# Entry of the first batch, order of the last batch and PReLU on Pool in a four-layer fused kernel

## The chip, the cores and the metric

One core of a Trainium2 chip runs the whole program. Its engines are PE (TensorE, matmuls), DVE (VectorE), ACT (ScalarE), POOL (GpSimd) and SP (SyncE, which here issues DMAs). The metric is the time of the device for one execution in microseconds, from the first to the last instruction on that core. Three runs are given for the kernel before, and one more execution was profiled.

## The reference

The input is 8 images of 512 channels and 32 x 32 = 1024 pixels, in fp32. Four layers follow each other, all of 1x1 convolutions:

```python
# layer 0: attention normalised by the largest singular value
f_x = relu(batchnorm(conv1x1(x, Wf, bf))); g_x = relu(batchnorm(conv1x1(x, Wg, bg)))
h_x = conv1x1(x, Wh, bh)                          # 64 channels each; batch statistics
attn = einsum('bcn,bcm->bnm', f_x, g_x) / sigma   # sigma: largest singular value
x = conv1x1(einsum('bnm,bcm->bcn', attn, h_x), Wv, bv) + x
# layer 1: group norm, softmax attention over 1024 pixels, 512 channels, residual
# layer 2: softmax attention with 128 channels, a batch norm, residual
# layer 3: signs of x times signs of W
y = einsum('bchw,oc->bohw', sign(x + rsign_bias), sign(W) * mean(abs(W)))
s = batchnorm(y) + x
t = s - pr_shift
out = where(t > 0, t, pr_slope * t) + pr_bias     # PReLU
```

## The kernel before

A tile of x is 128 partitions x 4 channel blocks (`cc`) x 1024 pixels; a "half" is 512 pixels. One fp32 matmul of the program shows as two instructions in the trace.

**Start (lines 1128 to 1187).** For each image the loop loads x in four blocks, and PE multiplies it by the weights of f, g and h (`products(i, cc)`, with i = 0, 1, 2; line 1157). For the first image the loop goes over the blocks and, in each, over f, g and h; for the others over f, g, h and then the blocks. x has two buffers, so the load of image b+2 waits for PE's work on image b. The small row tensors (`bg_row`, `bvc`, `bhc`, `wv2`, lines 194 to 204) are loaded by POOL's queue at the very beginning. The weights are loaded by SP's queue between the images.

**Middle (about 97 to 201 us).** The singular values come from a chain of small products (`chain`), and `filler()` yields other PE work in small items (weight products, transposes, Gram matrices) that are put between its steps. PE's order here is written out by hand (`manual_schedule`). At its end `entering(0)` brings in the first batch of the second part: `enter` yields after each of four channel blocks (matmul L396, then on DVE L405 and the statistics L408, L409), then after the two products of the group norm (L416, L423). Two filler items are put after each of the four blocks, and six after each of the other two steps. The last filler item is the product L1197 that makes `wo`.

**Entry.** The pools of the first part are closed, the pool `late` is opened (its tile `ones2` is filled by a DVE memset, L1375), then `normal` (lines 435 to 447) normalises the first batch, by halves, on DVE and ACT in turn; `split_h` makes differences of it on DVE (L312 to L315), and `make_u` multiplies (L373). A big product is done in the seven-product form of Strassen and Winograd (`seven`): sums and differences of quarters, seven products and additions of results. In it the first product is copied out of its bank by ACT (L335) before the fifth may accumulate onto that bank. Then `sums_of` makes the sums of quarters of `wo` and of the layer-2 weights on DVE.

**Batches (`fast`, lines 826 to 927).** Eight times: layer-1 scores (`scores1`), values, layer 2 (`project2`, `scores2`, `values2`, `close2`), layer 3 (`leave`). Steps of the next batch fill the gaps. `inverse_sums` sums the exponentials by a matmul with `ones2` (L788), takes the reciprocal on DVE (L796) with one half on each side of 64 partitions, and spreads it by four DMAs (L800); two more bring a row of it into `guard`, whose values `count_bad` examines on DVE (L737 to L747) at the end; the verdict `bad` decides whether a general path is run. In `leave` each output block takes a PSUM eviction with the residual (L700, DVE), a Relu (L704, ACT), a scaling with a bias (L705, ACT), a sum (L712, DVE) and the DMA to the output (L715, SP). The last batch takes the two signs of the weights unpacked (`signs`), has no next batch to fill its gaps, and ends the program.

Order of the engines: apart from PE's hand-written stretch, a scheduler places the instructions of each engine in a queue, which then runs in that order.

Of the kernel before, what the change touches and what calls it, by code (L numbers as in the profile page):

```python
# [83 lines left out]
def kernel(  # L84
# [109 lines left out]
    bg_row = const.tile([P, P], F32, tag="bg_row", name="bg_row")  # L194
    nc.gpsimd.dma_start(out=bg_row, in_=rows[MID + C :].partition_broadcast(P))

    bvc = const.tile([P, CC], F32, tag="bvc", name="bvc")
    nc.gpsimd.dma_start(out=bvc, in_=rows[MID : MID + C].rearrange("(cc p) -> p cc", p=P))
    bhc = const.tile([P, 1], F32, tag="bhc", name="bhc")
    wv2 = const.tile([P, C], F32, tag="wv2", name="wv2")  # L200
    for i in range(2):
        both = side(i)
        nc.gpsimd.dma_start(out=bhc[both, :], in_=rows[0:MID].rearrange("(p o) -> p o", o=1))
        nc.gpsimd.dma_start(out=wv2[both, :], in_=w_v0)
    minus_half = const.tile([P, CC], F32, tag="minus_half", name="minus_half")
# [36 lines left out]
    sa3 = const.tile([P, CC], F32, tag="sa3", name="sa3")  # L242
    cb3 = const.tile([P, CC], F32, tag="cb3", name="cb3")
    inv2 = const.tile([P, CC], F32, tag="inv2", name="inv2")
    bb2 = const.tile([P, CC], F32, tag="bb2", name="bb2")
# [49 lines left out]

    def sums_of(a, more):

        a11, a12, a21, a22 = a
        s1, s2, s4 = more
        tt = nc.vector.tensor_tensor  # L300
        tt(s1, a21, a22, ALU.add)
        tt(s2, s1, a11, ALU.subtract)  # L302
        tt(a21, a11, a21, ALU.subtract)
        tt(s4, a12, s2, ALU.subtract)
        return {"A11": a11, "A12": a12, "A22": a22, "S1": s1, "S2": s2, "S3": a21, "S4": s4}
# [128 lines left out]

    def normal(env, xt, by_halves=False):

        sc, bi = norm
        ht = env["big"].tile([P, CC, N], F32, tag="h", name="h")
        for ns in [half(h) for h in range(NH)] if by_halves else [slice(0, N)]:
            for cc in range(CC):  # L440
                s1, b1 = sc[:, cc : cc + 1], bi[:, cc : cc + 1]
                hs, xs = ht[:, cc, ns], xt[:, cc, ns]
                if cc % 2:
                    nc.scalar.activation(hs, xs, AF.Identity, bias=b1, scale=s1)
                else:
                    nc.vector.tensor_scalar(hs, xs, s1, b1, ALU.mult, ALU.add)
        return ht
# [214 lines left out]
    def leave(env, xt, dst, halves=range(NH), signs=None, stop=False):  # L662
# [3 lines left out]
        for h in halves:  # L666
# [7 lines left out]
            for j in range(CC // 2):  # L674
# [15 lines left out]
                if signs is None:  # L690
                    ps = product(sw3)
                    nc.scalar.activation(y2, ps, AF.Identity, bias=round3, scale=1.0 / PACK)
                    nc.vector.tensor_scalar(y2, y2, ROUND, None, ALU.subtract)
                    nc.vector.scalar_tensor_tensor(y1, y2, -PACK, ps, ALU.mult, ALU.add)
                    sums = y1, y2
                else:
                    sums = [product(lt) for lt in signs]

                for y, ps, oc in ((y1, sums[0], j), (y2, sums[1], j + 2)):
# [3 lines left out]
                    up = small.tile([P, HF], F32, tag="half_a", name="up3")  # L703
                    nc.scalar.activation(up, y, AF.Relu, bias=cb3[:, oc : oc + 1])  # L704
                    nc.scalar.activation(  # L705
                        y,
                        y,
                        AF.Identity,
                        bias=pb3[:, oc : oc + 1],
                        scale=col("L3_conv_pr_slope", oc),  # L710
                    )
                    nc.vector.scalar_tensor_tensor(  # L712
                        y, up, ps3[:, oc : oc + 1], y, ALU.mult, ALU.add
                    )
                    nc.sync.dma_start(out=dst[:, oc, half(h)], in_=y)  # L715
                yield
# [12 lines left out]
    def count_bad(env):  # L729
# [6 lines left out]
        nbad = late.tile([g, 1], F32, tag="nbad", name="nbad")  # L736
        nc.vector.tensor_scalar(fine, guard, 1.0 / GUARD, None, ALU.is_gt)  # L737
        nc.vector.tensor_scalar(other, guard, GUARD, None, ALU.is_lt)
        nc.vector.tensor_tensor(fine, fine, other, ALU.mult)
# [44 lines left out]
    def inverse_sums(env, esum, row):  # L784
# [21 lines left out]
        return full  # L806

    def entering(n):

# [16 lines left out]
    def fast(env, n, hb, ua):  # L826
# [14 lines left out]
        for k, _ in enumerate(scores1(env, hb, ua, es)):  # L841
            if rest3 and k % 2 == 0:
                if next(rest3[0], "end") == "end":
                    rest3.pop()
                    if more and order[n + 1] not in resident:
                        resident[order[n + 1]] = load_x(order[n + 1])
            if k == 8 and more:
                ahead = entering(n + 1)
# [57 lines left out]
        values2(0, range(0, 2))  # L906
        r = inverse_sums(env, esum, B + n)
        values2(0, range(2, NTH))
        att = values2(0, range(NTH, NT))
        values2(1, range(0, NTH))  # L910
        close2(xt, att, 0)
        att = values2(1, range(NTH, NT))
        count = iter(()) if more else count_bad(env)
        next(count, None)
        fill()
        for _ in leave(env, xt, dst, [0], signs):
            fill()
        close2(xt, att, 1)
        rest3.append(leave(env, xt, dst, [1], signs, more))
        if more:  # L920
            next(rest3[0])
        fill(2)
        for _ in steps:
            pass
        if not more:
            for _ in rest3.pop():
                next(count, None)

# [146 lines left out]
    def scale_signs(total):  # L1075
# [28 lines left out]
        nc.vector.tensor_tensor(pb3, slope, cb3, ALU.mult)  # L1104
        nc.vector.tensor_tensor(pb3, pb3, vec("L3_conv_pr_bias"), ALU.add)

    def scale_z():
# [39 lines left out]
    for b in range(B):  # L1147
        xt = load_x(b) if b else first
        for name, src, pool in later.get(b, ()):
            load_w(name, src, shapes.get(name, [P, CC, C]), pool)  # L1150
        if b >= B - 2:
            resident[b] = xt
# [12 lines left out]
        if b == 0:  # L1165
            for cc in range(CC):
                for i in range(3):
                    products(i, cc)
        for i in range(3):
            if b == B - 1 and i == 2:  # L1170
                for _ in natural("q", "w3"):
                    pass
            if b:
                for cc in range(CC):
# [182 lines left out]
    with tc.manual_schedule(engines={mybir.EngineType.PE}):  # L1357
# [7 lines left out]
        for k in range(CC + 2):  # L1365
            next(steps)
            for _ in range(2 if k < CC else 6):
                next(todo, None)
# [3 lines left out]

    late = ctx.enter_context(tc.tile_pool(name="late", bufs=1))
    ones2 = late.tile([P, P], F32, tag="ones2", name="ones2")
    nc.vector.memset(ones2, 1.0)  # L1375
    guard = late.tile([2 * B * 4, NH, P], F32, tag="guard", name="guard")
    bad = late.tile([1, 1], I32, tag="bad", name="bad")

    with ExitStack() as main:
# [9 lines left out]
        ua = got[0]  # L1389
        weights["o"] = sums_of(quarters_of(wo, chunks, cols2), [so[:, i] for i in range(3)])  # L1390
        sp = late.tile([P, 3, 2, P], F32, tag="sp", name="sp")
        tp = quarters_of(sbw["tpg"], chunks, [slice(0, P), slice(P, 2 * P)])
        weights["tp"] = sums_of(tp, [sp[:, i] for i in range(3)])
        for n in range(B):
# [172 lines left out]
```

## Time and profile before

| | us |
|---|---|
| median of three runs | 1938.97 (1938.92 to 1940.28) |
| span of the profiled execution | 1940.4 |
| PE busy | 1909.5 |
| DVE busy | 1149.8 |
| ACT busy | 513.6 |
| POOL busy | 224.1 |
| first matmul starts | 4.35 |
| last sign product ends on PE | 1928.8 |
| last DVE instruction ends | 1935.2 |

A line of the timeline gives the start, the duration, the engine, the line, the operation, output<-input, shape and count; in brackets stands the idle time of the engine before it and what ended that. A line of the waits gives engine, own line, what it waited for, the total, the number of times and the longest. Busy PE includes matmuls at half rate, so it must also be asked how far apart matmuls start.

### The profile page before, as it was taken

What the parts mean: (1) busy time and instruction counts of PE and PEld (TensorE: products, weight loads), DVE (VectorE), ACT (ScalarE), POOL (GpSimd) and SP (SyncE); (2) the same over time, 40 slices, a digit from 0 to 9 for tenths busy, and PEclk for the clock granted to TensorE, in tenths of its full rate; (3) what the DMA queues carried; (4) which work ended last, traced back from release to release, by engine and by line L of the source; (5) the groups of instructions that cost most, each with busy time, mean ns of one, the idle gap of its engine ahead of it and who ended that gap; (6) DMA issues with size and microseconds to landing.
All of it is one profiled execution on the core that took longest, in us unless ns stands there. A gap on an engine that the chain in (4) does not pass through costs nothing.

```text
span 1940.4 us, 16698 instructions
## 1 busy us (share of the span) xinstructions
PE 1909.5 (98%) x6230; PEld 984.6 (51%) x6230; DVE 1149.8 (59%) x1867; ACT 513.6 (26%) x815; POOL 224.1 (12%) x176
## 2 busy tenths in 40 slices
PE   8999999999999999999999999999999999999997
PEld 2367447544655447454555446544645455544653
DVE  2255578448864587637754677348663775466545
ACT  2141222124221432025212331034202421133014
POOL 1000001200112001200111011201120011101120
PEclk9999999999999999999999999999999999999999
DMA  8420000002000110002000120002000200010001
GB/s 308 163 77 7 1 6 12 1 11 87 17 1 1 33 65 17 1 10 89 15 2 1 33 71 11 1 11 87 11 0 1 86 14 9 0 33 22 11 1 57
DMA packets 27289, 67.00 MB, mean 35 GB/s; under 512 B 3824, under 2 KB 4592, under 8 KB 26560
## 3 DMA queue, kind: packets, MB, share of 16 engines
q1 hardware_dynamic: 26112, 65.09, 9.9%
q8 instruction: 51, 0.84, 0.2%
q0 software_dynamic: 224, 0.33, 0.1%
q10 hardware_dynamic: 864, 0.43, 0.1%
q14 instruction: 38, 0.31, 0.1%
HBM read 38.51 MB, written 18.87 MB: 30 GB/s over the span
## 4 chain that ended last, share of the span: by engine, by line
PE 89%; DVE 8%; ACT 1%; issue 1%; DMA 0%; ACTq 0%; POOL 0%; DVEq 0%
PE bank L373 40%; PE bank L540 20%; PE bank L890 6%; PE bank L767 6%; PE bank L1157 4%; PE bank L641 3%; PE bank L396 2%; PE bank L658 1%; PE wide L1197 1%; PE bank L944 1%; DVE both L712 1%; DVE both L700 1%; PE bank L945 1%; PE bank L788 1%; PE wide L1244 1%
## 5 line engine op out<-in xcount | busy, mean ns | idle before, releaser
L540 PE MATMUL bank<-e,vt 128*128 128x512 f32 x768 | 334.0, 593 | 0.0
L540 PEld LDWEIGHTS bank<-e,vt 128*128 128x128 f32 x768 | 145.2, 190 | 175.2 <-issue 173.0
L373 PE MATMUL bank<-ut,h 128*128 128x512 f32 x384 | 181.3, 596 | 0.0
L330 DVE TENSOR_TENSOR e<-bank,e 128x512 f32<-128x512 f32 x128 | 87.7, 685 | 65.2 <-PE bank L373 64.5
L373 PE MATMUL bank<-us,hs 128*128 128x512 f32 x256 | 122.1, 599 | 1.3 <-DVE us L302 0.5
L373 PEld LDWEIGHTS bank<-ut,h 128*128 128x128 f32 x384 | 71.6, 190 | 85.7 <-issue 83.5
L890 PE MATMUL bank<-e,tpg 128*128 128x512 f32 x256 | 114.6, 596 | 0.0
L767 PE MATMUL bank<-tpg 128*128 128x512 f32 x256 | 114.6, 592 | 0.0
L774 ACT ACTIVATE e<-bank 128x512 f32<-128x512 f32 x128 | 76.4, 597 | 128.6 <-PE bank L767 128.6
L373 PE MATMUL bank<-h,wu 128*128 128x512 f32 x192 | 90.7, 594 | 2.2 <-ACT ut L335 1.5
L345 POOL TENSOR_TENSOR e<-e 128x512 f32<-128x512 f32 x32 | 44.0, 1375 | 419.6 <-ACT e L324 419.6
L373 PE MATMUL bank<-wo,h 128*128 128x256 f32 x384 | 91.8, 382 | 0.0
L779 DVE TENSOR_TENSOR esum<-esum,e 128x1024 f32<-128x1024 f32 x48 | 58.8, 1225 | 54.8 <-ACT e L774 54.8
L330 DVE TENSOR_TENSOR vt<-bank,vt 128x512 f32<-128x512 f32 x64 | 44.1, 689 | 70.5 <-PE bank L373 70.1
L890 PEld LDWEIGHTS bank<-e,tpg 128*128 128x128 f32 x256 | 48.0, 190 | 63.9 <-issue 63.9
L767 PEld LDWEIGHTS bank<-tpg 128*128 128x128 f32 x256 | 48.6, 190 | 60.7 <-issue 60.5
L373 PEld LDWEIGHTS bank<-wo,h 128*128 128x128 f32 x384 | 71.6, 190 | 13.4 <-ACT vt L324 4.1
L345 POOL TENSOR_TENSOR ut<-ut 128x512 f32<-128x512 f32 x16 | 21.8, 1360 | 483.0 <-ACT ut L326 483.0
L373 PEld LDWEIGHTS bank<-us,hs 128*128 128x128 f32 x256 | 46.8, 190 | 56.0 <-issue 46.3
L669 ACT ACTIVATE sg<-xt,rb 128x512 f16<-128x512 f32 x64 | 45.2, 718 | 104.4 <-DVE xt L660 100.9
L796 DVE RECIPROCAL rsum<-bank 128x512 f32<-128x512 f32 x16 | 53.7, 3358 | 30.3 <-PE bank L788 30.3
L1157 PE MATMUL bank<-xt,fg 128*64 128x512 f32 x256 | 60.3, 616 | 4.4 <-DMA fg<-in_w_fg 4.4
(320 smaller groups left out, 3080.4 us busy)
## 6 DMA issues: line engine op xcount, KB each, us to landing
xt<-in_x SPq DMA_DIRECT2D x55, 512.0 KB
out<-both SPq DMA_DIRECT2D x64, 256.0 KB
rfull<-rsum SPq DMA_DIRECT2D x64, 128.0 KB
f_dram<-f SPq DMA_DIRECT2D x8, 256.0 KB
fb<-f_dram SPq DMA_DIRECT2D x8, 256.0 KB
w<-in_w SPq DMA_DIRECT2D x1, 1024.0 KB
q<-in_w_q SPq DMA_DIRECT2D x1, 1024.0 KB
k<-in_w_k SPq DMA_DIRECT2D x1, 1024.0 KB
```

Source lines behind the costliest of these rows:

```text
L330: nc.vector.tensor_tensor(dst, ps, u, ALU.add)
L345: nc.gpsimd.tensor_tensor(c22, c22, c12, ALU.add)
L373: mm(out=ps[:, q * w : (q + 1) * w], lhsT=lt(ka, kb, q, k), rhs=rhs(ka, kb, q, k), start=first and q == 0 and k == 0, stop=last and k == 1 ...
L540: mm(out=ps, lhsT=a[:, t, bass.ts(r_, P)], rhs=e[t], start=first and t == 0, stop=last and t == NTH - 1, skip_group_check=True,)
L641: mm(out=ps[:, i, :], lhsT=xt[:, cc, bass.ts(4 * h + i, P)], rhs=sbw["tpg"][:, cc, 2 * P : 3 * P], start=cc == 0, stop=cc == CC - 1,)
L669: nc.scalar.activation(sg[:, cc, :], xt[:, cc, half(h)], AF.Sign, bias=rb3[:, cc : cc + 1])
L767: mm(out=ps, lhsT=pt[:, 0, bass.ts(t, P)], rhs=tt[:, 0, half(h)], start=True, stop=True,)
L774: nc.scalar.activation(e[:, half(h)], ps, AF.Exp, scale=float(P) ** -0.5)
L779: nc.vector.tensor_tensor(esum, esum, e, ALU.add)
L796: nc.vector.reciprocal(r, ps)
L890: mm(out=banks[h], lhsT=gt[:, t, :], rhs=es[t][:, half(h)], start=t == 0, stop=t == NT - 1,)
L1157: mm(out=banks[i][side(h), :], lhsT=w0[i][:, cc, :], rhs=xt[:, cc, half(h)], start=cc == 0, stop=cc == CC - 1,)
```

## The change

1. For the first image PE does all f and g products before the h products.
2. The row loads, except `bhc`, move from POOL's queue at the start to SP's queue at image 4.
3. At the entry, three filler items instead of two stand after each channel block, five instead of six after the other two steps; `normal` for the first batch runs on DVE alone; the `late` pool waits for single tiles of the memory it takes over and no longer for the whole; `sums_of` for `wo` and for the layer-2 weights moves into the first batch's `scores1`, after its steps 2 and 6.
4. The last batch: the reciprocals are taken for all 128 partitions in two instructions (`inverse_rows`), without the spreading DMAs; the second half's products, the closing of the halves, the guard count and the two halves of `leave` stand in another order.
5. Of the last batch's eight outputs, six take PReLU as a maximum with `nc3` = -`cb3` times `ps3` (one DVE instruction), a scaling with bias `qb3` on ACT, and a sum on POOL. The seventh stays; the eighth is done and stored in two quarters.

The core of the diff:

```diff
-    nc.gpsimd.dma_start(out=bg_row, in_=rows[MID + C :].partition_broadcast(P))
-    nc.gpsimd.dma_start(out=bvc, in_=rows[MID : MID + C].rearrange("(cc p) -> p cc", p=P))
-        nc.gpsimd.dma_start(out=wv2[both, :], in_=w_v0)
+    def load_rows():
+        nc.sync.dma_start(out=bg_row, in_=rows[MID + C :].partition_broadcast(P))
+        nc.sync.dma_start(out=bvc, in_=rows[MID : MID + C].rearrange("(cc p) -> p cc", p=P))
+        for i in range(2):
+            nc.sync.dma_start(out=wv2[side(i), :], in_=w_v0)
...
-                if cc % 2:
+                if cc % 2 and not alone:
                     nc.scalar.activation(hs, xs, AF.Identity, bias=b1, scale=s1)
                 else:
                     nc.vector.tensor_scalar(hs, xs, s1, b1, ALU.mult, ALU.add)
...
+                    if signs is not None and (h == 0 or j == 0):
+                        nc.vector.tensor_scalar(
+                            up, y, nc3[:, oc : oc + 1], ps3[:, oc : oc + 1], ALU.max, ALU.mult
+                        )
+                        nc.scalar.activation(
+                            y, y, AF.Identity, bias=qb3[:, oc : oc + 1],
+                            scale=col("L3_conv_pr_slope", oc),
+                        )
+                        nc.gpsimd.tensor_tensor(y, y, up, ALU.add)
+                        nc.sync.dma_start(out=dst[:, oc, half(h)], in_=y)
+                        continue
+                    final = signs is not None and y is y2
+                    for q in (slice(0, HF // 2), slice(HF // 2, HF)) if final else [slice(0, HF)]:
...
+    def inverse_rows(env, esum, row):
+        full = env["small"].tile([P, NH, HF], F32, tag="rfull", name="rfull", bufs=1)
+        for h in range(NH):
+            ps = bank()
+            mm(out=ps, lhsT=ones2, rhs=esum[:, half(h)], start=True, stop=True)
+            nc.vector.reciprocal(full[:, h, :], ps)
...
+            if n == 0 and k == 2:
+                weights["o"] = sums_of(quarters_of(wo, chunks, cols2), [so[:, i] for i in range(3)], True)
+            if n == 0 and k == 6:
+                tp = quarters_of(sbw["tpg"], chunks, [slice(0, P), slice(P, 2 * P)])
+                weights["tp"] = sums_of(tp, [sp[:, i] for i in range(3)], True)
...
+            r = inverse_rows(env, esum, B + n)
+            att = values2(0, range(2, NT))
+            values2(1, range(0, 2))
+            close2(xt, att, 0)
+            values2(1, range(2, 6))
+            before, after = leave(env, xt, dst, [0], signs), leave(env, xt, dst, [1], signs)
+            count = count_bad(env)
+            next(count)
+            next(before)
+            next(before)
+            att = values2(1, range(6, NT))
+            next(before)
+            close2(xt, att, 1)
+            for _ in before:
+                pass
+            next(after)
+            next(count)
+            for _ in after:
+                pass
...
+        nc.vector.tensor_scalar(nc3, cb3, -1.0, None, ALU.mult)
+        nc.vector.tensor_tensor(qb3, cb3, vec("L3_conv_pr_bias"), ALU.add)
...
+        if b == 4:
+            load_rows()
...
         if b == 0:
             for cc in range(CC):
-                for i in range(3):
+                for i in range(2):
                     products(i, cc)
...
-            if b:
+            if b or i == 2:
                 for cc in range(CC):
                     products(i, cc)
...
-            for _ in range(2 if k < CC else 6):
+            for _ in range(3 if k < CC else 5):
                 next(todo, None)
...
-    late = ctx.enter_context(tc.tile_pool(name="late", bufs=1))
+    late = ctx.enter_context(tc.tile_pool(name="late", bufs=1, reuse_waits="tile"))
```

## The prediction

> **What bounds the kernel.** I read the page's busy table and slices first, then the list of waits of PE, then the timeline at three places. PE is busy 98% of the span, so a change can gain only where PE stands still, where it runs slowly, or behind its last matmul.
>
> ```profile
> span 1940.4 us, 16698 instructions
> PE 1909.5 (98%) x6230; PEld 984.6 (51%) x6230; DVE 1149.8 (59%) x1867; ACT 513.6 (26%) x815; POOL 224.1 (12%) x176
> PE   8999999999999999999999999999999999999997
> ...
> PE bank L1157 <- DMA fg<-in_w_fg: 4.4, 1, 4.4
> PE bank L416 <- DVE mv L415: 3.5, 5, 1.8
> PE bank L396 <- ACT pv L282: 1.6, 4, 0.7
> PE bank L373 <- ACT ut L335: 1.5, 1, 1.5
> PE bank L1157 <- DMA h<-in_w_h: 1.4, 1, 1.4
> PE bank L681 <- ACT sg L669: 1.1, 1, 1.1
> ...
> PE bank L373 <- DVE h L446: 0.7, 1, 0.7
> ```
>
> PE's idle time is 1940.4 - 1909.5 = 30.9 us. The first slice (8) and the last (7) hold most of it; the named waits are each a microsecond or two. All lie at the start, at the entry of the first fast batch (180 to 206 us) or in the last batch: the three places which the diff edits.
>
> The start, PE and its weight loads:
>
> ```profile
> 4.35 4.30 PE L1157 MATMUL bank<-xt,fg 128*64 128x512 f32 x8 [4.35 <-DMA fg<-in_w_fg]
> 10.02 1.98 PE L1157 MATMUL bank<-xt,h 128*64 128x512 f32 x4 [1.37 <-DMA h<-in_w_h]
> ...
> 10.02 0.30 PEld L1157 LDWEIGHTS bank<-xt,h 128*64 128x64 f32 x4 [3.05 <-DMA h<-in_w_h]
> ```
>
> The page's 1.37 us understates this: the weight loads stop for 3.05 us, and matmul ends are modelled. Eight instructions follow each other every 0.43 us (4.35 to about 7.8), then PE waits for h until 10.02. From 10.02 the spacing is again 0.43 us, until about 14.0; then it is 0.215 us. So PE runs at half rate twice.
>
> The end:
>
> ```profile
> 1919.88 3.60 PE L658 MATMUL bank<-att,z 128*128 128x512 f32 x8
> 1926.10 0.67 DVE L660 TENSOR_TENSOR xt<-bank,xt 128x512 f32<-128x512 f32 x1
> 1927.99 2.73 DVE L700 SCALAR_TENSOR_TENSOR both<-bank,sa,xt 128x512 f32<-128x512 f32 x4 [1.16 <-PE bank L681]
> 1934.47 0.75 DVE L712 SCALAR_TENSOR_TENSOR both<-up,ps,both 128x512 f32<-128x512 f32 x1 [0.71 <-ACT both L705]
> ```
>
> PE finishes the second half's L658 products at 1923.5, but DVE adds the last of them only at 1926.1-1926.8, since it stands behind L700, L712 and the guard count. The last matmul ends at 1928.8, the last DVE instruction at 1935.2, and 5.2 us of output DMA and closing follow.
>
> [...]Here L345 takes 1.26 us on POOL and a comparable add on DVE (L330) 0.69. [...]the trace has 0.41 us (L446) against 0.69.[...]
>
> **Part by part.** The base is the profiled span of 1940.4; the three timed runs are 1938.92 to 1940.28, so I subtract the sum from the median 1938.97.
>
> *Start.* The f and g products of all four channel blocks come first, h last. PE has 16 f/g products (32 instructions) before it needs h, landed by 10.02. From 4.35 it goes on at 0.43 us;[...] First case: 9 slow instructions, 39 at 0.215 = 8.4, end 16.7. Second: 14 slow, 34 fast = 7.3, end 17.8. Before, batch 0 ended at 20.5. Gain 2.7 to 3.8; I take 3.2. It needs x on time: the windowed traffic sums to about 1.6 MB by 8 us and 2.3 MB by 11, of which 0.3 MB (two w_v0 loads, the bias rows) now leave the start. Block 1 is needed at 7.8, when fg and x blocks 0 and 1 are 1.25 MB: it fits narrowly. The next batches need PE 11.04 us each and their x came early, so the gain is kept.
>
> *Row loads on SP.* Four issues at batch 4, about 0.35 to 0.8 us each (shortest and longest output issue), 1.4 to 3.2 us in SP's queue behind x of batch 4. Behind them wait z, tpg and x of batch 5, whose issue waits for PE until 53.8; SP had issued tpg by 45.9, so 7.9 us are free. Cost 0. First use of wv2 is at 168 us. The two new 128x4 operations (nc3, qb3; 0.16 us each) lie in DVE's early idle time: 0.
>
> *Entry of the first batch.* Three filler items instead of two between the L396 steps put about 4 us of PE work between them against 3.1 to 3.4 us of DVE work (two L405 at 0.73, two L408 at 0.69, L409, mask). The 1.83 us before L416 goes, perhaps 0.1 stays: 1.7. The memset of ones2 no longer waits for PE (it ended DVE's 6.96 us wait at 201.35). The built order shows DVE going from the norm directly into eight normalisations: 3.0 us of norm chain + 0.2 + 8 x 0.41 = 6.5, beside the 16 L1197 instructions then left (7.0 us). So 0.7 of L446's wait goes. ACT no longer normalises (2.93 us from 202.2), so L335 copies at once: the gap between the first two L373 products shrinks from 205.65 - 201.99 - 1.72 = 1.94 to copy plus handovers, 0.58 + 0.15 = 0.73: 1.2. The sums of wo no longer stand among DVE's hs differences: 0.3 on the next product. Together 3.9; I take 3.8.
>
> *Sums moved into scores1.* Four at 0.69 and four at 0.42 = 4.4 us of DVE. In the built order the first four stand where DVE was idle for 4.92 us (236.1 to 241.1); the others delay esum and one L330 by under 1.7 us, while PE has eight banks. Cost 0, at most 1.7. PE's order in all middle batches is unchanged.
>
> *The last batch.* Two full reciprocals replace one and the broadcast DMA: DVE 1901.4 + 2 x 3.36 = 1908.1, while the page has the broadcast's att at 1908.23. Even, but PE puts fewer products before closing the first half: close from 1908.9 instead of 1909.6. The count (2.3 us) then stands before the first L700, filling until PE has the first sign product (1916.0). From there I count DVE by its queue. Four outputs of the first half at 0.73 + 0.44 (maximum and scaling); att of the second half done at 1919.3; L660 of the second half 1920.7 to 1923.7, against 1926.8 before: 3.1 earlier. ACT's signs end at 1924.4, PE's last product at 1927.6, L700 of the last output at 1929.0. For each output treated the new way ACT loses a Relu (0.71), DVE trades L712 (0.74) for 0.44, POOL takes 1.26. The last POOL sum ends about 1930.7, before the last two outputs, which keep the old way: Relu and Identity in quarters, last DVE instruction at about 1932.3 (1935.2 before). That is 2.9. A last transfer of 128 instead of 256 KB gains 0 to 0.5 (256 KB at 257 GB/s is 1.0). SP's wait for the verdict comes at 1925.5, before its fourth output is ready. End: 3.0, range 1.5 to 3.6.
>
> Sum: 3.2 + 3.8 + 3.0 = 10.0. 1938.97 - 10.0 = 1929.0.
>
> **Rivals.** *A late x.* If a block of x lands late at 7.8 to 12 us, PE pauses again[...]: start gain 1. For it: a narrow fit. Against: 0.3 MB less traffic. 1931.2.
>
> *POOL in the chain.* If POOL's sums slow DVE's maximum or their results come late (six at 1.26, the sixth must beat 1932.3), the end gains nothing: 1932.0. Against: POOL's additions keep 1.26 us in the median beside a busy DVE; for: their longest is 2.18.
>
> *Entry lost.* If the moved sums hold L330 up and stall PE, or h still waits, the 3.8 falls to 0: 1932.8.
>
> *Slower: SP blocked by the row loads.* bvc is written as 512 separate four-byte elements. If the four loads hold SP longer than its free 7.9 us plus about 2 us of slack in x of batch 5, PE starves. Slower needs the 10 us of gain eaten as well and 4 more: 24 us or more in that queue, then 1943. Against: from POOL they landed within 7.4 us.
>
> *The change does not do it.* Two of the above together: about 1935.5, no change.
>
> **Chances.** Forecast 0.64, late x 0.14, POOL 0.10, entry lost 0.04, two together 0.04, slower 0.04. Range 1926.5 to 1932.5: the low end is the top of the three ranges (3.8 + 3.9 + 3.6 = 11.3[...]), the high end takes in late x and POOL. 0.2% (3.9 us) is about what a measurement can tell; it is passed below 1935.1. Faster 0.92, same 0.04, slower 0.04.
>
> **What would show it.** Right: no pause of PE's loads at 7.8, slow spacing over by 10.5, batch 1 starting at 16.7 to 17.8; no L416 wait; the first two L373 products under 1 us apart; last DVE instruction 3 us nearer the last L788 than before (1935.2 - 1900.7 = 34.5). Wrong: a DMA wait in the first 13 us, new waits between 230 and 260, POOL as releaser of the last output, a span over 1935.

## The result, and the profile after

| | before | after |
|---|---|---|
| median time, us (runs) | 1938.95 (4; 1938.84 to 1940.28) | 1932.34 (4; 1931.48 to 1932.70) |
| ratio, 95% interval | | 0.9964 [0.9946, 0.9981] |
| span of the profiled execution | 1940.4 | 1930.8 |

The changed kernel is 6.6 us faster by the medians, the two profiled spans are 9.6 us apart. Both differences are true. The execution of the kernel before whose profile is shown took 1942.25 us, 3.3 more than the median, the profiled one of the changed kernel 1932.70.

The page of the changed kernel, its busy table and PE's slices:

```profile
span 1930.8 us, 16673 instructions
PE 1906.6 (99%) x6230; PEld 987.4 (51%) x6230; DVE 1158.2 (60%) x1875; ACT 507.7 (26%) x807; POOL 229.7 (12%) x178
PE   9999999999999999999999999999999999999997
```

PE's idle time is 1930.8 - 1906.6 = 24.2 us, against 30.9 before. That is 6.7 of the 9.6 us; the other 2.9 are busy time, which fits products that PE made at half rate before (0.43 us apart until about 14.0 us, 0.215 after). The first slice is a 9 now, the last is still a 7.

PE's list of waits, after (own line, what it waited for, total, times, longest):

```profile
PE bank L1225 <- DMA fg<-in_w_fg: 4.5, 1, 4.5
PE bank L423 <- DVE mv L422: 2.2, 5, 0.6
PE bank L403 <- ACT pv L287: 1.6, 4, 0.7
...
PE bank L380 <- ACT ut L342: 0.7, 1, 0.7
```

L423 is the old L416: its longest wait is 0.6, not 1.8. L380 is the old L373: its wait for the first half's copy is 0.7 instead of 1.5, and the 0.7 for the normalised halves (old L446) is no longer there, nor is the wait for h (1.4) or that of the second sign product (1.1).

The start of the changed kernel, PE's weight loads:

```profile
4.53 0.29 PEld L1225 LDWEIGHTS bank<-xt,fg 128*64 128x64 f32 x2 [4.53 <-DMA fg<-in_w_fg]
...
7.78 0.46 PEld L1225 LDWEIGHTS bank<-xt,fg 128*64 128x64 f32 x2 [0.40 <-issue]
...
9.48 0.46 PEld L1225 LDWEIGHTS bank<-xt,fg 128*64 128x64 f32 x2 [0.40 <-issue]
10.15 0.25 PEld L1225 LDWEIGHTS bank<-xt,fg 128*64 128x64 f32 x2 [0.21 <-issue]
```

Two loads follow in 0.85 us until 9.9 and in 0.43 from 10.15: the half rate ends once and for good. There is no pause at 7.8, where PE stood 3.05 us before.

The end of the changed kernel, the timeline of DVE (L709 is the PSUM eviction, L715 the maximum, L739 the sum of the old form), then that of POOL:

```profile
1913.20 0.98 DVE L715 TENSOR_SCALAR up<-both,nc,ps 128x512 f32<-128x512 f32 x1
...
1919.12 0.55 DVE L715 TENSOR_SCALAR up<-both,nc,ps 128x512 f32<-128x512 f32 x1
1919.58 1.40 DVE L709 SCALAR_TENSOR_TENSOR both<-bank,sa,xt 128x512 f32<-128x512 f32 x2
1920.90 1.40 DVE L715 TENSOR_SCALAR up<-both,nc,ps 128x512 f32<-128x512 f32 x1
1922.23 0.74 DVE L709 SCALAR_TENSOR_TENSOR both<-bank,sa,xt 128x512 f32<-128x512 f32 x1
1923.89 2.27 DVE L739 SCALAR_TENSOR_TENSOR both<-up,ps,both 128x512 f32<-128x512 f32 x3 [0.93 <-ACT both L732]
```

```profile
1911.37 2.52 POOL L725 TENSOR_TENSOR both<-both,up 128x512 f32<-128x512 f32 x2 [44.44 <-ACT both L718]
...
1919.22 2.80 POOL L725 TENSOR_TENSOR both<-both,up 128x512 f32<-128x512 f32 x2 [2.70 <-ACT both L718]
1923.23 1.27 POOL L725 TENSOR_TENSOR both<-both,up 128x512 f32<-128x512 f32 x1 [1.21 <-ACT both L718]
```

PE's last sign product ends at about 1920.8, but its eviction, the last L709, starts only at 1922.23: it stands behind a maximum that takes 1.40 us instead of 0.55, and POOL works on a sum until 1922.02 beside it. The other long maximum (0.98, from 1913.20) lies beside POOL's sums up to 1913.89.

All profiles of this study can be laid over each other by four lengths read off the timelines: S, from the start of the span to the start of the first product of the second image (batch 1); M, from there to the start of the last product of the exponentials' sums (L788 before, L842 after); E, from there to the end of the last DVE instruction; T, the rest to the end of the span. S + M + E + T is the span.

| kernel | S | M | E | T | mean time less that of before, timed beside it |
|---|---|---|---|---|---|
| before | 20.51 | 1880.21 | 34.50 | 5.18 | |
| after | 17.56 | 1875.75 | 32.85 | 4.64 | |
| before, repeated | 18.45 | 1880.16 | 34.51 | 5.18 | -0.1 |
| order of f, g, h alone | 18.87 | 1880.17 | 34.51 | 5.15 | -0.2 |
| row loads alone | 16.52 | 1880.54 | 34.51 | 5.13 | -1.3 |
| order and row loads | 17.44 | 1878.82 | 34.51 | 4.93 | -1.8 |
| entry alone | 18.43 | 1875.52 | 34.51 | 4.84 | -3.6 |
| filler counts alone | 22.06 | 1877.88 | 34.52 | 5.14 | -0.9 |
| end alone | 22.42 | 1880.10 | 32.85 | 4.93 | -1.6 |
| after, repeated | 16.80 | 1875.73 | 32.85 | 4.42 | -8.2 |
| after, repeated again | 17.86 | 1875.76 | 32.84 | 4.74 | -7.3 |
| after without the new PReLU | 16.83 | 1875.76 | 33.62 | 4.59 | -7.4 |
| after, sums on DVE | 16.86 | 1875.77 | 34.01 | 4.46 | -6.8 |
| after, sixth maximum later | 16.23 | 1875.81 | 32.34 | 4.52 | -7.9 |

E repeats to 0.01 us and M nearly so; S scatters. T is the rest of a span given to 0.1 us, so it is good to 0.05. Means are given since the times of the kernel before lie in groups, and a median jumps from one to the next. One caution for S: in kernels with moved row loads that first product is recorded 0.3 us earlier against what follows it (the first transposes L1053 come 7.28 after it, otherwise 6.96), so 0.3 of their smaller S comes back in M.

From before to after: S -2.95, M -4.46, E -1.65, T -0.54, together the 9.6.

### The profile page after: what moved, and what is told of

It reads as the page before. It is cut to its first block, busy times and chain, and to the rows that moved or that the text cites. A ratio compares the mean times of both kernels' runs of the same rounds, so it can differ in the third digit from the quotient of the medians.

```text
span 1930.8 us, 16673 instructions
## 1 busy us (share of the span) xinstructions
PE 1906.6 (99%) x6230; PEld 987.4 (51%) x6230; DVE 1158.2 (60%) x1875; ACT 507.7 (26%) x807; POOL 229.7 (12%) x178
## 3 DMA queue, kind: packets, MB, share of 16 engines
HBM read 38.51 MB, written 18.87 MB: 30 GB/s over the span
## 4 chain that ended last, share of the span: by engine, by line
PE 91%; DVE 7%; ACT 1%; issue 1%; DMA 0%; POOL 0%; DVEq 0%; ACTq 0%
PE bank L380 41%; PE bank L547 20%; PE bank L937 6%; PE bank L796 6%; PE bank L1225 4%; PE bank L648 3%; PE bank L403 2%; PE bank L665 2%; PE bank L1008 1%; PE wide L1265 1%; DVE both L739 1%; DVE both L709 1%; PE bank L1009 1%; PE wide L1312 1%; PE bank L688 1%; PE bank L817 1%
## 5 line engine op out<-in xcount | busy, mean ns | idle before, releaser
L380 PE MATMUL bank<-ut,h 128*128 128x512 f32 x384 | 181.3, 596 | 0.0
L380 PE MATMUL bank<-us,hs 128*128 128x512 f32 x256 | 122.1, 599 | 1.3 <-DVE us L309 0.5
L380 PEld LDWEIGHTS bank<-ut,h 128*128 128x128 f32 x384 | 71.5, 190 | 85.8 <-issue 83.6
L380 PE MATMUL bank<-wo,h 128*128 128x256 f32 x384 | 91.8, 382 | 0.0
L380 PE MATMUL bank<-h,wu 128*128 128x512 f32 x192 | 90.3, 593 | 0.7 <-ACT ut L342 0.7
L380 PEld LDWEIGHTS bank<-wo,h 128*128 128x128 f32 x384 | 71.6, 190 | 13.5 <-ACT vt L331 4.1
L380 PEld LDWEIGHTS bank<-us,hs 128*128 128x128 f32 x256 | 46.7, 190 | 56.0 <-issue 46.4
```

The costliest lines, as they stand in the source:

```text
L380: mm(out=ps[:, q * w : (q + 1) * w], lhsT=lt(ka, kb, q, k), rhs=rhs(ka, kb, q, k), start=first and q == 0 and k == 0, stop=last and k == 1 ...
```

## The experiments

**The kernel before, repeated.** No edit.

> The kernel before once more, unchanged. The change took 9.6 us from the profiled span (1940.4 to 1930.8) but only 6.6 us from the time. Theory A (the profiled execution of before was itself slow: in it the TensorE clock was 0.62 and 0.53 of full speed from 184 to 188 us, right after PE's wait before L416): a new profile has a span of about 1937 to 1938.5, and the clock dip at 184 to 188 us is absent in it or shorter. Theory B (the dip belongs to every execution, and the change loses 3 us in its timed runs that its profile does not have): the new profile again shows about 1940.4 with the dip. Time in both: 1938.9, ratio 1.000.

Measured: 1939.90 us median of 13 runs, ratio 0.9999 [0.9991, 1.0007], span 1938.3. M and E are those of the first profile to 0.05 us; only S differs, 18.45 for 20.51. h landed at much the same time (9.81 and 10.02), but here PE went on at full rate at once (two weight loads every 0.43 us from 10.29), there only 4 us later. So 2 us of the profile that the prediction was read from are not a fixed property of the kernel. The fall of the clock is in this profile too (0.61 and 0.53 in the two windows from 182 to 186), so each theory has one half of it: the shorter span is A's, the fall that stays is B's.

**Start: the order alone.**

```diff
-                for i in range(3):
+                for i in range(2):
                     products(i, cc)
...
-            if b:
+            if b or i == 2:
```

> Only the order of the first image's products (f and g first, h last); the row loads stay on POOL at the start. The changed kernel has batch 1 starting at 17.56 us against 20.51, so the start gives 2.95 us in the profiles. If the order alone does it: 2.5 to 3.2 us less, no pause of PE's weight loads at 7.8 us. If the order needs the row loads out of the way (late x): PE waits for a block of x or for fg between 7.8 and 12 us, and 1 us or less is gained.

Measured: 1939.58 us, ratio 1.0000 [0.9992, 1.0009]. PE's weight loads:

```profile
8.01 0.51 PEld L1157 LDWEIGHTS bank<-xt,fg 128*64 128x64 f32 x4 [1.20 <-issue]
...
9.34 0.25 PEld L1157 LDWEIGHTS bank<-xt,fg 128*64 128x64 f32 x2 [0.18 <-issue]
11.95 0.20 PEld L1157 LDWEIGHTS bank<-xt,fg 128*64 128x64 f32 x4 [2.37 <-DMA xt<-in_x]
```

PE no longer waits for h, it waits 2.37 us for x instead. The new order by itself only changes what is late; the second expectation held.

**Start: the row loads alone.**

```diff
-    nc.gpsimd.dma_start(out=bg_row, in_=rows[MID + C :].partition_broadcast(P))
...
-    nc.gpsimd.dma_start(out=bvc, in_=rows[MID : MID + C].rearrange("(cc p) -> p cc", p=P))
...
-        nc.gpsimd.dma_start(out=wv2[both, :], in_=w_v0)
...
+        if b == 4:
+            load_rows()
```

> Of the start's edits only the row loads (to SP at image 4); f, g and h keep their order by blocks. The order alone gained nothing (1939.58 against 1939.84) since x came late; both edits together gave 1938.16. Theory 'the row loads only make room in the start, the gain comes from not waiting for h': the wait for h stays, 1 to 2 us long, and the time is within 0.6 us of the kernel before. Rival 'the row loads alone are what held the start up': h or x lands 1 us or more earlier, and the time equals that of both edits, 1937.9 to 1938.5.

Measured: 1938.34 us, ratio 0.9995 [0.9986, 1.0003]; means 1938.29 against 1939.57. The interval of the ratio includes 1, so what speaks here is the trace and, more weakly, the means. `load_rows` holds the same loads, issued by SP. The wait for h is nearly gone though the order is the old one:

```profile
7.04 0.23 PEld L1162 LDWEIGHTS bank<-xt,fg 128*64 128x64 f32 x1 [0.41 <-issue]
7.57 0.51 PEld L1162 LDWEIGHTS bank<-xt,h 128*64 128x64 f32 x3 [0.30 <-DMA h<-in_w_h]
```

The DMA view of 2 to 8 us, first of the kernel before, then of this one (packets, MB and mean rate; then by queue: packets, MB, share of the 16 engines):

```profile
DMA packets 1185, 1.53 MB, mean 256 GB/s; under 512 B 181, under 2 KB 779, under 8 KB 1185
...
q1 hardware_dynamic: 425, 1.06, 48.1%
q0 software_dynamic: 92, 0.12, 24.9%
```

```profile
DMA packets 1346, 1.91 MB, mean 318 GB/s; under 512 B 211, under 2 KB 851, under 8 KB 1346
...
q1 hardware_dynamic: 546, 1.51, 68.4%
...
q0 software_dynamic: 64, 0.00, 0.6%
```

In the kernel before, POOL's queue (q0) moved 8% of the bytes (0.12 of 1.53 MB) and held the 16 DMA engines for 24.9% of these 6 us, which is 1.5 us. Without it the loads of x, f, g and h moved 0.45 MB more in the same time, and h landed by 7.57 instead of 10.02. The theory written down for this run (the loads only make room, the wait for h stays) fell; the rival held.

**Start: both.** The two diffs above together.

> Parts 1 and 2 of the change together, nothing else: f and g products first, and the row loads at image 4 on SP. With the order alone x was late (PE waited 1.49 us for x at 11.96). Theory 'the row loads made x late, the two edits only work together': no DMA wait of PE in the first 13 us, batch 1 starts at 16.7 to 18.0 in the profile, time 2 to 3 us below the kernel before (about 1937.3 against 1939.8), and the times scatter less. Rival [...]the time equals before within 1 us and batch 1 starts anywhere between 17.5 and 22. In both, the 1.8 us wait at L416 and the dip of the clock behind it remain.

Measured: 1938.16 us, ratio 0.9991 [0.9983, 0.9999]; means 1938.13 against 1939.94. No wait for a DMA but the first ones; S = 17.44. Together the edits gained 1.8 in the mean, the row loads alone 1.3, the order alone 0.2: what the order adds to the row loads is less than these means can tell. The expected scatter came true (1937.46 to 1939.08 against 1937.77 to 1942.20 of before), the expected 2 to 3 us did not quite.

The two last kernels also settled something about the entry. Both have the same wait of 1.8 us before the group norm's product (L419 here), and M differs by 1.72. By windows of 2 us (busy time and count of PE, PEld, DVE, ACT, POOL, then the clock granted to PE, DMA share, GB/s), row loads alone, then both edits:

```profile
182.00:184.00 2.00, 2.00 (x3) 0.78 (x3) 0.29 (x1) 0.00 (x0) 0.00 (x0) 0.50 0.00 0
184.00:186.00 2.00, 2.00 (x4) 0.76 (x3) 0.00 (x0) 0.00 (x0) 0.00 (x0) 0.68 0.00 0
```

```profile
182.00:184.00 2.00, 2.00 (x11) 1.29 (x11) 0.89 (x6) 0.00 (x0) 0.00 (x0) 1.00 0.00 0
184.00:186.00 2.00, 2.00 (x6) 0.95 (x5) 0.00 (x0) 0.00 (x0) 0.00 (x0) 1.00 0.00 0
```

In one the clock fell to half behind the wait for 3.4 us (which costs 1.7), in the other it stayed. PE is "busy" in both.

**Entry alone.**

```diff
-                if cc % 2:
+                if cc % 2 and not alone:
...
+            if n == 0 and k == 2:
+                weights["o"] = sums_of(...)
+            if n == 0 and k == 6:
...
-            for _ in range(2 if k < CC else 6):
+            for _ in range(3 if k < CC else 5):
...
-    late = ctx.enter_context(tc.tile_pool(name="late", bufs=1))
+    late = ctx.enter_context(tc.tile_pool(name="late", bufs=1, reuse_waits="tile"))
```

> Only the entry of the first batch (filler items 3 and 5, normalisation on DVE, the late pool by tile, the sums moved into scores1). The profiles have 4.4 us between the first L396 and the third product of the entry (38.5 less 34.1 us from 167.33 and 169.97). Theory A: about 1.8 us of that is the clock dip, which the timed runs of before mostly do not have, so the time falls by 2.0 to 3.0 us. Theory B: the time falls by 4.0 to 4.6 us.

Measured: 1936.74 us, ratio 0.9983 [0.9975, 0.9990]; means 1936.22 against 1939.85. M falls by 4.64 against the repeated kernel before. 1.72 of that is the lowered clock behind the old wait, which is not in this profile; 2.9 are waits. The time fell by 3.1 (medians) or 3.6 (means), between the two theories: more than the waits alone, less than all of M.

**The filler counts alone.**

```diff
-            for _ in range(2 if k < CC else 6):
+            for _ in range(3 if k < CC else 5):
```

> Of the entry's edits only the filler counts: three items after each channel block and five after the other two steps, on the kernel before. The whole entry gained 3.1 us in its median (3.6 in its mean). Theory 'the counts remove the wait before the group norm's product (1.83) and, in the executions in which it makes the clock fall, the dip behind it (about 1.7); the rest of the entry's gain is the waits of the first L373 products': no wait of PE over 1 us at 180 to 186, clock 1.00 from 182 to 192, third L373 product 1.7 to 2.2 earlier counted from batch 1's start, where the waits of 0.73 and 1.46 stay; time 1.7 to 2.6 below the kernel before. Rival 'the items put in earlier are missing later': the pause moves behind the second step of the group norm or to the first L373 product, and the gain is under 1 us.

Measured: 1937.88 us, ratio 0.9993 [0.9985, 1.0001]; means 1938.65 against 1939.57. PE's waits between 171 and 202 us:

```profile
PE bank L373 <- DVE h L446: 0.7, 1, 0.7
PE bank L396 <- ACT pv L282: 0.7, 1, 0.7
PE bank L416 <- DVE mv L415: 0.6, 1, 0.6
```

The 1.83 became 0.61, the clock stayed at 1.00, and M fell by 2.28. Less the 1.72 of the clock, that is 0.56: not the whole 1.22 of the shorter wait. Most of the rest sits in the second block's L396 products, which took 1.92 us here and 1.45 in the kernel with both start edits; what they met there I did not find. The other 2.36 of the entry's 4.64 belong to the other edits: the first L373 comes 0.91 earlier, the second follows it after 2.56 instead of 3.66 us (1.10), and the next 0.2 sooner. In the times the counts gained less than expected (0.9 in the mean, 1.1 in the median, with a ratio whose interval includes 1; 1.7 to 2.6 were written down). That fits executions in which the clock doesn't fall. An estimate of their number comes from the entry: its means differ by 3.63, of which 2.92 are waits, and (3.63 - 2.92) / 1.72 puts the fall in some 0.4 of the executions. The scatter of the means leaves this uncertain by 0.2; five of the six profiles with the wait show the fall, too few to set against it.

**End alone.** Parts 4 and 5 of the change, nothing of parts 1 to 3.

```diff
+            r = inverse_rows(env, esum, B + n)
...
+                    if signs is not None and (h == 0 or j == 0):
+                        nc.vector.tensor_scalar(up, y, nc3[...], ps3[...], ALU.max, ALU.mult)
+                        nc.scalar.activation(y, y, AF.Identity, ...)
+                        nc.gpsimd.tensor_tensor(y, y, up, ALU.add)
```

> Only the last batch (reciprocals of all partitions, the joined order, PReLU with POOL's sums). In the profiles 39.7 us lie between the start of the last L788 and the end of the span, and 37.5 us in the changed kernel: 2.2 us less expected in the time, if the end does not depend on the other parts. The forecast had 3.0 us; if its count of DVE was right and the profile is an accident, 3.0.

Measured: 1938.16 us, ratio 0.9991 [0.9985, 0.9998]; means 1938.22 against 1939.85. E = 32.85, the same as in the whole change and 1.66 less than before. The time fell by 1.6 to 1.7, less than either of the two figures written down (2.2 and 3.0). Its span of 1940.3 is no loss: S is 22.42 in that execution, the largest seen.

**The new PReLU taken out again.**

```diff
-                    if signs is not None and (h == 0 or j == 0):
+                    if False:
```

> The changed kernel with all outputs of the last batch in the old form of PReLU (Relu and Identity on ACT, sum on DVE); the eighth is still done in quarters, and order, reciprocals, entry and start stay. Theory 'the maximum beside POOL costs DVE 0.55 us, with two outliers of 0.98 and 1.40, against 0.74 for the sum it replaces, so the new form saves nearly nothing': within 0.7 us of the whole change, and the last DVE instruction again 32.4 to 33.4 after the start of the last L842. Rival 'the new form is what gains at the end': 1.5 to 2.5 us slower than the whole change, last DVE instruction at 34.4 or later. A third, 'POOL stands in the way': faster by over 0.7.

Measured: 1932.67 us (1931.95 to 1933.00; 5 runs) against 1931.68 (1931.62 to 1932.01) of the whole change timed beside it; E = 33.62, 0.77 more. That lies between what the theory (under 0.7) and the rival (1.5 to 2.5) had said. But the edit does more than was written down: with the branch gone, the second output of every pair falls into the code for quarters, so four outputs of the last batch are done and stored in two quarters (eight stores of 128 KB in this profile, two in the changed kernel), not the eighth alone. What the extra quarters cost was not measured apart, so 0.77 is not the worth of the new form alone. The other 0.9 of E is the order, the reciprocals and the eighth output's quarters.

**The sums on DVE.**

```diff
-                        nc.gpsimd.tensor_tensor(y, y, up, ALU.add)
+                        nc.vector.tensor_tensor(y, y, up, ALU.add)
```

> The changed kernel with the six sums of the last batch's outputs on DVE in place of POOL. Theory 'POOL's sums slow DVE's two-fold maximum[...]': every maximum now takes the same 0.44 to 0.55 us, none 0.98 or 1.40. Rival 'the outliers are waits of DVE's own (for the copy before, or for ACT)': one or two of the six still take about 1 us or more. On the end: six more sums at 0.69 are 4.1 us of DVE work, of which the two or three of the second half stand in the way of the last output: 1.0 to 2.5 us slower than the whole change.

Measured: 1933.25 us (1932.46 to 1933.67), E = 34.01. The instructions on the tile `up` at the end (duration min/median/max in ns), first of the changed kernel, then of this one:

```profile
L715 DVE TENSOR_SCALAR up<-both,nc,ps x6: 545/546/1404, 1909.8 to 1920.9; 128x512 f32<-128x512 f32 x6
L725 POOL TENSOR_TENSOR both<-both,up x6: 1267/1272/1575, 1911.4 to 1923.2; 128x512 f32<-128x512 f32 x6
...
L739 DVE SCALAR_TENSOR_TENSOR both<-up,ps,both x3: 484/486/1154, 1923.9 to 1925.7; 128x256 f32<-128x256 f32 x2, 128x512 f32<-128x512 f32 x1
```

```profile
L715 DVE TENSOR_SCALAR up<-both,nc,ps x6: 537/542/546, 1909.1 to 1922.3; 128x512 f32<-128x512 f32 x6
...
L739 DVE SCALAR_TENSOR_TENSOR both<-up,ps,both x3: 483/484/752, 1924.4 to 1926.2; 128x256 f32<-128x256 f32 x2, 128x512 f32<-128x512 f32 x1
```

With POOL idle no maximum takes over 0.55 us, and the sum of the old form takes 0.75, not 1.15. So the long ones are POOL's doing, as the theory had it. The two long maxima (0.98 and 1.40 us) end 0.29 and 0.28 us after POOL's sum ends (1914.18 after 1913.89, 1922.30 after 1922.02), the long L739 (1.15 us) 0.55 after (1925.05 after 1924.50). By what means POOL holds them up the trace doesn't show. The other way round, POOL's sum that began 0.1 us after a maximum took 1.58 us instead of 1.27. The evictions L709, with one input in PSUM, keep 0.74 to 0.75 us beside POOL. Even so, sums on DVE are 1.16 us worse in E and 1.57 in the medians, within the expected 1.0 to 2.5: POOL's help makes these three DVE instructions up to 1.7 us longer (0.43 + 0.85 + 0.40) and is still worth it.

**The whole change, twice more.** No edit to it.

> The whole change again, on the same chip as its parts. Sum of the parts: entry 3.1 to 3.6, end 1.7, start 2 to 3, so 6.8 to 8.3 below the kernel before: about 1932.3 against 1939.8. Theory 'the three parts add up': it lies in that range, and batch 1 again starts at 16.7 to 18.0. Rival 'the start's gain and the entry's are partly the same one': under 6 us, above 1934.

> The whole change once more, for the comparison in this call: 1931.5 to 1932.7, as in its two earlier measurements; last DVE instruction 32.85 after the start of the last L842, in each profile; the start of batch 1 is the only stage that may move, between 16.7 and 18.0.

Measured: 1931.68 us, ratio 0.9957 [0.9943, 0.9971], and 1932.55 us, ratio 0.9962 [0.9949, 0.9976]. S was 16.80 and 17.86, as expected; everything between S and the last DVE instruction is the same to 0.03 us. The parts sum to 1.8 + 3.6 + 1.6 = 7.0 in the means, the whole gained 8.2 and 7.3: they add up within what can be told.

**The sixth maximum behind all evictions.** In the second half of the last batch the sixth output's maximum, scaling and sum are issued after both evictions L709 of the last pair and after the seventh output.

```diff
+                if signs is not None and h and j:
+                    raw(*pairs[0])
+                    tc.keep_in_program_order(raw(*pairs[1]))
+                    with_dve(y1, j, False)
+                    for d in held:
+                        with_pool(*d)
+                    with_dve(y2, j + 2, True)
```

> The changed kernel, and in the second half of its last batch the sixth output's maximum, ACT scaling and POOL sum stand behind all four evictions L709, so that the maximum (1.40 us beside POOL's sum) no longer delays the eviction of the last output. Theory 'the last output's chain starts 1.4 us after its product only because of that maximum': that eviction starts within 0.3 us of its product, the last DVE instruction lies 31.4 to 32.1 after the start of the last L842 (32.85 in the changed kernel), and the time is 0.6 to 1.3 below the whole change in this call. Rival 'ACT's chain of the last two outputs, or POOL's late sixth sum, then sets the end': within 0.5 of the whole change, POOL or SP being the releaser of the last transfer.

Measured: 1931.76 us (1930.82 to 1932.22; 5 runs), ratio to before 0.9961 [0.9948, 0.9975], against 1932.55 (1931.51 to 1933.01) of the whole change timed beside it. DVE at the end:

```profile
1918.31 2.06 DVE L743 SCALAR_TENSOR_TENSOR both<-bank,sa,xt 128x512 f32<-128x512 f32 x3
1920.29 0.74 DVE L711 TENSOR_SCALAR up<-both,nc,ps 128x512 f32<-128x512 f32 x1
1921.41 0.75 DVE L736 SCALAR_TENSOR_TENSOR both<-up,ps,both 128x512 f32<-128x512 f32 x1 [0.38 <-ACT both L729]
1923.40 0.98 DVE L736 SCALAR_TENSOR_TENSOR both<-up,ps,both 128x256 f32<-128x256 f32 x2 [1.24 <-ACT both L729]
```

The evictions now run without a gap, as the theory had it, but E fell by 0.51 and not by 0.75 to 1.45: DVE then waits 1.24 us for ACT, whose chain of scalings and Relus sets the end. This is what the rival said, and in E about the 0.5 us that it allowed. The version is ahead of the changed kernel by 0.5 us in E and by 0.6 in the mean time; five runs each, which overlap, don't establish the latter.

## Why the prediction was right or wrong

The forecast of a gain was right, and 1932.34 lies in its range, but only 0.16 us below the upper end (the lower end, 1926.5, holds about 1 us more than the three ranges add up to, an estimate that nothing measured supports); of the two repeats one (1931.68) lies in it and one (1932.55) just outside. The point value of 1929.0 was 3.3 us too low. By the parts alone, in mean times: start 1.8 for 3.2, entry 3.6 for 3.8, end 1.6 for 3.0, together 7.0 for 10.0. That the two profiles lie 9.6 apart, close to the sum, is partly luck.

*Base.* The gains were read from the profile of an execution that took 1942.25 us and subtracted from a median of 1938.97. I set the span of 1940.4 beside the timed runs as if both measured the same; in every run here the time is 1.7 to 2.0 us more than the span, so the profiled execution was slower than all those timed. Its start was late (S = 20.51; 18.45 when repeated), and the forecast counted that as a gain of every execution. I take the start's missing 1.4 us to lie here. That is argued: S was 18.43 to 22.42 in five profiles with the old start and row loads, too few for a mean.

*Start, 3.2.* The size fits the pair of profiles (2.95, of which 0.3 comes back in M), and what should show it is there: no pause, full rate from 10.15, S = 17.56. The 9 or 14 slow instructions it counted with were an estimate; the eight profiles with moved row loads have 9 to 15 weight loads at the half rate, the changed kernel's own 15. The reason given failed. It was "PE has 16 f/g products before it needs h"; the order alone gained nothing and made x late, and the row loads alone removed the wait for h. The term that was mis-sized is "0.3 MB now leave the start": the loads were counted in bytes, 8% of the traffic in the window, and held the DMA engines for 24.9% of it.

*Late x.* This rival, 1931.2, described a true danger, shown by the order alone. With the row loads gone it costs little: in one of the three profiles of the changed kernel PE's weight loads wait 0.38 us for x at 11.60, where their usual gap there is 0.18; in the other two they don't.

*Row loads on SP.* Cost 0 holds: M contains no new wait of PE, and the rival of a blocked SP found nothing.

*Entry, 3.8.* M fell by 4.46, and the agreement is partly luck. "The 1.83 us before L416 goes, perhaps 0.1 stays: 1.7" failed: 0.61 stays, and the counts are worth 0.56 net of the clock. The first pair of L373 products (1.2 forecast, 1.10 measured), L446 (0.7 forecast; 0.73 of wait gone) and the differences (0.3 forecast, 0.2 measured) were right. What the forecast lacked altogether is the clock behind that wait, 1.72 us. It could be read in the profile of before, in the windows of 2 us after that wait:

```profile
184.00:186.00 2.00, 1.74 (x9) 1.74 (x10) 0.86 (x7) 0.00 (x0) 0.00 (x0) 0.62 0.00 0
186.00:188.00 2.00, 2.00 (x6) 1.08 (x6) 0.29 (x1) 0.00 (x0) 0.00 (x0) 0.53 0.00 0
```

The prediction considered half rate only in the first 14 us. "Entry lost" did not happen.

*Sums moved to scores1.* Cost 0 holds: the first product of `us` and `hs` comes 7.27 us earlier than before (223.72 for 230.99), the last product of the exponentials' sums 7.41.

*Last batch, 3.0.* E and T fell by 1.65 and 0.54 in the pair of profiles, 2.2 together; the end alone gave 1.6 in the mean time. "That is 2.9" for the last DVE instruction is the step that failed: it was 1.65. Counted from the last L788 or L842, the last eviction was forecast at 28.28 (1929.0 - 1900.72) and came at 28.92; of six maxima priced at 0.44 (the mean spacing of L446 in the profile of before) four held DVE for 0.46 to 0.55, the two beside POOL for 0.90 and 1.33. Behind it 3.3 were forecast and 3.93 measured, where the late sixth output's scaling on ACT stands ahead of the last two's and L739 took 1.15 beside POOL.

*POOL in the chain.* What this rival named is there (two maxima of 0.98 and 1.40 us beside POOL's sums, 0.55 at most without), its price was not: the end still gains 1.6 to 2.2 of the 3.0, and 0.77 of it went with the new form (and the extra quarters) when that was taken out. POOL is not the releaser of the last output.

## What to carry to other kernels

Ask which of its executions a profile shows before its gaps are subtracted from a median: the time of that execution stands beside it, and what the clock did in it may be missing from many of the others. Price a load in a crowded start by the share of the DMA engines that its queue held and not by its bytes, and look at the granted clock behind a pause of PE such as the 1.83 us here. At the start that column is no help: it reads 1.00 all through it, while matmuls follow at half rate (six in 12 to 14 us of the profile of before, twelve in 14 to 16), so go by the spacing. Work handed to POOL cost DVE nothing here beside the evictions L709, which read PSUM (0.74 to 0.75 us); beside a maximum in SBUF, or a sum with both inputs there, one of the two engines took longer (maxima 0.98 and 1.40 us for 0.55, the sum 1.15 for 0.75, POOL's sum 1.58 for 1.27). So put the instruction that the end hangs on first.

## What was not expected of the hardware

- A pause of PE of 1.82 to 1.83 us was followed by half the granted clock in five of the six profiles that have it, for 3.4 us, at a cost of 1.7; in the sixth, with both start edits, the clock stayed at 1.00. In the profile of before the pause lies from 182.43 to 184.26 and the half clock from 184.46 to 187.87, while PE is at work again. Why the one of the sixth profile (179.67 to 181.49) was spared is not shown. With the filler counts alone the wait there is 0.61 us and the clock 1.00.
- The start scatters. With nothing in PE's way the full rate came 3.2 to 5.7 us after the first product (eight profiles with moved row loads), and S was 16.2 to 17.9. With the pause for h it came at once (at 9.8), 4 us or 6 us after PE went on, and S was 18.4 to 22.4. What sets that moment is not shown. I take the scatter, with the fall behind the pause, to be why 53 executions of the kernel before lie in groups near 1938.2, 1940.0 and 1942.4 while those of the changed kernel keep within 1931.5 to 1933.0. It fits that the entry alone, whose profile has the pause for h but no fall, has two groups, 1934.7 to 1935.5 (eight times) and 1936.7 to 1937.6 (nine). All this is argued from profiles, each of which shows one execution, and not shown.
- The shortest instruction of a line is not its price. The prediction read 0.41 us for the scaling with a bias (L446, fp32, from SBUF to SBUF). That is the first of four in the profile of before; the other three took 0.54, as did all eight of the same line (L453) in the changed kernel, and the maxima beside an idle POOL. First the four of before, then the eight:

```profile
201.44 1.78 DVE L446 TENSOR_SCALAR h<-xt,r_r,bi 128x512 f32<-128x512 f32 x4
192.18 3.74 DVE L453 TENSOR_SCALAR h<-xt,r_r,bi 128x512 f32<-128x512 f32 x8
```

They follow each other every 0.46 us, so the time on record overlaps that of the next one. That spacing is what a queue of them costs.
